# Routed experts on one Trainium2 core: three row tiles an expert, with ten slots for fourth tiles

## The chip, the cores and the metric

The kernel runs on one core of one Trainium2 chip. The metric is the device time of one execution in microseconds. Three runs of the kernel before gave 2011.19, 2011.19 and 2011.78; the median is 2011.19. The profile comes from one further execution.

## The reference

3125 nodes with 256 features go through four residual layers: a three-layer graph attention, a routed expert layer, a graph sum, and a top-1 expert layer. Only the second is touched by the change:

```python
logits = jnp.einsum('bsd,de->bse', x, gate_w) + gate_b          # 16 experts
probs = jax.nn.softmax(logits, axis=-1)
top_probs, top_idx = jax.lax.top_k(probs, 2)                    # two experts a node
top_probs = top_probs / jnp.sum(top_probs, axis=-1, keepdims=True)
h1 = jnp.einsum('bsd,edh->bseh', x, w1)                         # 256 -> 512
h2 = jnp.einsum('bsd,edh->bseh', x, w2)
hidden = jax.nn.silu(h1) * h2
expert_out = jnp.einsum('bseh,eho->bseo', hidden, w3)           # 512 -> 256
```

The output is the sum of each node's two expert outputs with their weights, added to `x`. Each node counts twice, so 6250 rows are spread over 16 experts, on average 390.6 an expert.

## The kernel before

**Routing.** During the last attention layer `Router` computes every group's gates and scatters each normalised row, with its node number and its weight in two further columns, to its expert's place in the DRAM table `rows0` (3200 rows are set aside for each expert). The first 512 rows of every expert are filled beforehand with spare rows (`spare_rows`), whose node number points to spare rows behind `sums`; so an expert may be read as four full tiles of 128 whatever its count is. `Router.finish` takes the largest count to `over`; if an expert had more than 512 rows (`CAP0`), the kernel would run a general path at its end instead.

**Experts.** `routed_experts` loops over the 16 experts and treats all four tiles (`nq = 4`) of one at once:

- ACT's queue issues the loads of w1, w2 and w3 (512 KB each, L692 to L696, two buffers of each); SP's queue issues `xs`, the expert's 512 rows (L700, two buffers).
- DVE casts the node numbers to `who` (L702, two buffers). PE turns `xs` by eight transposes (L707), ACT copies them to `xsT` (L708).
- For each of four 128-wide quarters `j` of the hidden layer, PE multiplies w1 and then w2 with 512 columns of `xsT` (L715) into the PSUM tiles `ps_h1` and `ps_h2` (two buffers each). ACT takes the silu of the first (L718), DVE multiplies by the second into `hid` (L719).
- For each of the four row tiles PE multiplies `hid` with w3 (L723), DVE scales by the row's weight into `y` (L726, three buffers), and POOL issues an indirect DMA that adds the 128 rows into `sums` in DRAM at the rows in `who` (L728).

All products are float32, which PE runs as two passes each. The order of the instructions on an engine is made by the framework from the program's order and its estimates; the queues keep it. An instruction that waits on a semaphore holds up all behind it on its engine, DMA issues on ACT and SP included. In the order that was made, the cast `who` of an expert stands on DVE two experts ahead: the buffer it writes becomes free when the scatter-adds of the expert just finished have landed, and the first `hid` of the next expert stands behind it.

**After it**, the rows of `sums` are read back into `x` (L733) when all scatters have landed, and the graph sum begins. The last stage (`routed_top1`) reads 128-row tiles at places taken from a small table by register loads (L882, L884) and multiplies them (L895 transposes, L868 products); it is the model for the slots of the change and is itself not changed.

Of the kernel before, what the change touches and what calls it, by code (L numbers as in the profile page):

```python
# [9 lines left out]
F32 = mybir.dt.float32  # L10
F16 = mybir.dt.float16
BF16 = mybir.dt.bfloat16
I32 = mybir.dt.int32
# [8 lines left out]
P = 128  # L22
# [498 lines left out]
CAP0 = 512  # L521
CAP1 = 1024
# [20 lines left out]
def table(nc, pool, behind, func):  # L543

    one = pool.tile([P, 1], F32, name="table")
    nc.scalar.activation(one, behind[:, 0:1], func, scale=0.0, bias=1.0)
# [8 lines left out]
class Router:  # L555
# [6 lines left out]
    def __init__(self, tc, cp, ident, eps, iota, count, rows, sums, gate_w, gate_b):  # L562
        nc = self.nc = tc.nc
        self.tc, self.ident, self.eps, self.iota, self.rows, self.sums = tc, ident, eps, iota, rows, sums
# [105 lines left out]
    def finish(self, pp, over):  # L670

        total = pp.tile([1, NX0], F32, name="ps_z")
        self.nc.tensor.matmul(total, self.every[:, 0:1], self.pre[:, NT], start=True, stop=True)
        self.nc.vector.tensor_reduce(over, total, AX.X, OP.max)


def routed_experts(tc, x, ident, rows, sums, w1, w2, w3):
# [6 lines left out]
    nq = CAP0 // P  # L684
    with tc.tile_pool(name="rw", bufs=2) as ep, tc.tile_pool(name="rx", bufs=2) as xp, \
         tc.tile_pool(name="rs", bufs=3) as sp, \
# [3 lines left out]
        for e in range(NX0):  # L690
            a = ep.tile([P, KD, HID0], F32, name="w1")
            nc.scalar.dma_start(a, w1[e].rearrange("(k p) h -> p k h", p=P))  # L692
            b = ep.tile([P, KD, HID0], F32, name="w2")
            nc.scalar.dma_start(b, w2[e].rearrange("(k p) h -> p k h", p=P))
            o = ep.tile([P, nh, D], F32, name="w3")
            nc.scalar.dma_start(o, w3[e].rearrange("(k p) f -> p k f", p=P))  # L696
            xs = xp.tile([P, nq, ROW0], F32, name="xs")
            for q, n in ((0, nq),) if e else ((0, 1), (1, 1), (2, nq - 2)):
                at = e * NP + q * P
                nc.sync.dma_start(xs[:, q:q + n], rows[at:at + n * P].rearrange("(q p) f -> p q f", p=P))  # L700
            who = xp.tile([P, nq], I32, name="who")
            nc.vector.tensor_copy(who, xs[:, :, D])  # L702
            xsT = xp.tile([P, KD, CAP0], F32, name="xsT")
            for k in range(KD):
                ps = tp.tile([P, CAP0], F32, name="ps_x")
                for q in range(nq):
                    nc.tensor.transpose(ps[:, q * P:(q + 1) * P], xs[:, q, k * P:(k + 1) * P], ident)  # L707
                nc.scalar.copy(xsT[:, k], ps)  # L708
            hid = xp.tile([P, nh, CAP0], F32, name="hid")
            for j in range(nh):  # L710
                p1 = pp.tile([P, CAP0], F32, name="ps_h1")
                p2 = pp.tile([P, CAP0], F32, name="ps_h2")
                for ps, w in ((p1, a), (p2, b)):
                    for k in range(KD):
                        nc.tensor.matmul(ps, w[:, k, j * P:(j + 1) * P], xsT[:, k], start=(k == 0),  # L715
                                         stop=(k == KD - 1))
                s = sp.tile([P, CAP0], F32, name="silu")
                nc.scalar.activation(s, p1, AF.Silu)  # L718
                nc.vector.tensor_tensor(hid[:, j], s, p2, op=OP.mult)  # L719
            for q in range(nq):  # L720
                ps = po.tile([P, D], F32, name="ps_o")
                for j in range(nh):
                    nc.tensor.matmul(ps, hid[:, j, q * P:(q + 1) * P], o[:, j], start=(j == 0),  # L723
                                     stop=(j == nh - 1))
                y = sp.tile([P, D], F32, name="y")
                nc.vector.tensor_scalar(y, ps, xs[:, q, D + 1:D + 2], None, op0=OP.mult)  # L726

                independent(tc, f"sums{e}", nc.gpsimd.indirect_dma_start(  # L728
                    out=sums[:, :], out_offset=bass.IndirectOffsetOnAxis(ap=who[:, q:q + 1], axis=0),
                    in_=y, in_offset=None, bounds_check=NP + CAP0 - 1, oob_is_err=True, compute_op=OP.add))  # L730
        table(nc, sp, s, AF.Sqrt)
# [239 lines left out]
def dense_attention(tc, dram, counts, x_in, big, ident, eps, layers, src, dst, rows, high, make_router, over):  # L971
# [10 lines left out]
    with tc.tile_pool(name="dw", bufs=1) as cp, tc.tile_pool(name="dwl", bufs=2) as wl, \  # L982
# [9 lines left out]
        with tc.tile_pool(name="dp", bufs=8) as pmp, tc.tile_pool(name="ds", bufs=2) as sp, \  # L992
# [147 lines left out]
            router.finish(zp, over)  # L1140
# [283 lines left out]
def spare_rows(tc, cp, rows0, rows1):  # L1424
# [16 lines left out]
    to.append((rows1[NX1 * NP:], empty1))  # L1441
    return [lambda o=o, i=i: nc.sync.dma_start(o, i) for o, i in to], [empty0[:, 0, 0:1], empty1[:, 0:1]]
# [3 lines left out]
def routed(ctx: ExitStack, tc: tile.TileContext, i: dict, out: bass.AP, over):  # L1446
# [5 lines left out]
    rows0 = dram.tile([NX0 * NP, ROW0], F32, name="rows0")  # L1452
# [4 lines left out]
    early = ctx.enter_context(tc.tile_pool(name="early", bufs=1))  # L1457
    with tc.tile_pool(name="counts", bufs=1) as kp:
# [3 lines left out]
                                                            i["L0_ffn_gate_w"], i["L0_ffn_gate_b"]), over[:, 0:1])  # L1462
        with tc.tile_pool(name="s0", bufs=1) as sp:
            ws, wm = (two_halves(nc, sp, i["L1_gnn_" + n], "s_" + n) for n in "WM")
            hidden = hidden_weights(nc, early, *(i["L1_ffn_" + n] for n in ("W1", "b1", "Wg", "bg")), x[:, 0, 0:1])
            routed_experts(tc, x, ident, rows0, sums, *(i["L0_ffn_" + n] for n in ("w1", "w2", "w3")))
# [95 lines left out]
```

## Time and profile before

| | |
|---|---|
| median of 3 runs | 2011.19 us (2011.19 to 2011.78) |
| the profiled execution: its time | 2013.53 us |
| its span, and mean granted TensorE clock | 2011.8 us, 0.987 |
| the routed-expert stage in it | 1143 to 1501 us |
| busy in this stage of 358 us | PE 352.2, PEld 209.7, POOL 98.1, DVE 76.5, ACT 58.2 us |
| DMA in this stage | 46% of 16 engines, 107 GB/s |

The span is the time from the first to the last instruction of the profiled execution, and its time the whole of that execution; it was 2.34 us slower than the median of the unprofiled runs. PE is TensorE's products and PEld its weight loads, which run beside the products. A group's line gives the line of the kernel, engine, operation, destination and sources, shape, count, busy microseconds, the mean nanoseconds of one, and the idle time before it with what ended it. Ends of matmuls are modelled and one overlaps the next, so the time of a pass is read from start to start.

### The profile page before, as it was taken

How to read it: one execution, taken by the hardware profiler on the slowest of the kernel's cores; microseconds unless marked ns; L12 is line 12 of the kernel's file. 1: busy time of each engine (PE TensorE's matmuls, PEld its weight loads, DVE VectorE, ACT ScalarE, POOL GpSimd, SP SyncE). 2: the span in 40 equal slices, each digit the busy share in tenths (PEclk: the TensorE clock that was granted, in tenths of full speed). 3: DMA queues.
4: the chain of work that ended last, by engine and by line, in shares of the span. 5: the costliest groups of instructions: out<-in, count | busy, mean ns of one | idle time of the engine just before them, and what ended most of it. 6: DMA issues, size and time to landing. Idle time of an engine off the chain costs nothing. (4 is left out here: it accounts for less than half of the span.)

```text
span 2011.8 us, 27108 instructions
## 1 busy us (share of the span) xinstructions
PE 1899.9 (94%) x9234; PEld 1465.1 (73%) x9234; DVE 1004.2 (50%) x2900; ACT 756.7 (38%) x2242; POOL 287.1 (14%) x398
## 2 busy tenths in 40 slices
PE   2999999999999999999999699999989999997998
PEld 1788888887888888788888356556647887554887
DVE  5888978785444444577777322122226222323222
ACT  2867867672011111122222211111116999544221
POOL 1200000000000000032222223222320000132222
PEclk9999999999999999999999799999999999998999
DMA  4001112476000000111111345545531000633664
GB/s 127 25 1 64 33 64 116 191 281 259 30 0 1 1 1 6 37 43 43 43 43 39 126 110 124 133 105 125 118 60 47 1 1 1 220 157 143 199 208 132
DMA packets 97568, 173.82 MB, mean 86 GB/s; under 512 B 9814, under 2 KB 70581, under 8 KB 97392
## 3 DMA queue, kind: packets, MB, share of 16 engines
q1 hardware_dynamic: 59292, 109.03, 15.8%
q0 software_dynamic: 17264, 35.33, 6.7%
q10 hardware_dynamic: 20866, 27.63, 4.7%
q8 instruction: 76, 1.25, 0.3%
q14 instruction: 70, 0.57, 0.1%
HBM read 82.98 MB, written 91.35 MB: 87 GB/s over the span
## 5 line engine op out<-in xcount | busy, mean ns | idle before, releaser
L1089 PE MATMUL acc<-big,pm 128*128 128x257 f32 (+1 forms) x3750 | 868.1, 382 | 2.5 <-DVE pm L1086 2.1
L1089 PEld LDWEIGHTS acc<-big,pm 128*128 128x128 f32 (+1 forms) x3750 | 681.5, 187 | 108.9 <-DVE pm L1086 7.3
L1086 DVE SCALAR_TENSOR_TENSOR pm<-tau,rho,counts 128x256 f32<-128x256 f32 (+1 forms) x975 | 432.3, 469 | 137.0 <-PE acc L1089 135.1
L715 PE MATMUL ps_h<-xsT,w 128*128 128x512 f32 x512 | 226.5, 601 | 4.0 <-ACT xsT L708 4.0
L715 PEld LDWEIGHTS ps_h<-xsT,w 128*128 128x128 f32 x512 | 96.9, 192 | 124.3 <-issue 111.8
L1206 PE MATMUL acc<-msg,cr 128*128 128x512 f32 (+1 forms) x625 | 157.8, 404 | 0.0
L1405 DVE TENSOR_TENSOR ohk<-iota_k,key 128x1200 f16<-128x1200 f16 x196 | 152.4, 778 | 2.4 <-PE acc_c L1417 2.3
L1417 PE MATMUL acc_c<-ohk,ohs 128*128 128x200 f16 x1176 | 133.3, 251 | 4.9 <-DVE ohs L1405 2.4
L1202 ACT ACTIVATE cr<-counts 128x256 fp32r<-128x256 uint8 (+1 forms) x325 | 130.5, 402 | 19.3 <-DMA sums<-y,who 11.5
L728 POOL DMA_INDIRECT sums<-y,who x64 | 99.3, 1552 | 264.3 <-DVE y L726 249.6
L1206 PEld LDWEIGHTS acc<-msg,cr 128*128 128x128 f32 (+1 forms) x625 | 114.9, 185 | 28.9 <-ACT cr L1202 1.2
L1417 PEld LDWEIGHTS <-ohs 128*128 128x128 f16 x1176 | 105.9, 99 | 29.7 <-DVE ohs L1405 4.2
L1401 ACT ACTIVATE far<-iota_s,low 128x128 f16<-128x128 f16 x360 | 123.7, 398 | 6.3 <-DVE low L1373 1.8
L868 PE MATMUL ps_y<-t_wd,hsT 128*128 x512 | 118.4, 385 | 0.0
L723 PE MATMUL ps_o<-w,hid 128*128 128x256 f32 x512 | 113.1, 379 | 0.0
L723 PEld LDWEIGHTS ps_o<-w,hid 128*128 128x128 f32 x512 | 97.3, 190 | 20.1 <-issue 7.7
L1420 ACT CAST counts<-acc_c 128x400 uint8<-128x400 f32 x196 | 94.0, 479 | 45.4 <-PE acc_c L1417 44.6
L868 PEld LDWEIGHTS ps_y<-t_wd,hsT 128*128 128x128 f32 x512 | 96.5, 194 | 12.3
L718 ACT ACTIVATE silu<-ps_h 128x512 f32<-128x512 f32 x64 | 38.2, 597 | 162.7 <-PE ps_h L715 162.7
L719 DVE TENSOR_TENSOR hid<-silu,ps_h 128x512 f32<-128x512 f32 x64 | 43.8, 688 | 104.9 <-PE ps_h L715 104.8
L777 PE MATMUL ps_H<-big,t_w 128*128 128x512 f32 (+1 forms) x224 | 93.1, 552 | 0.7 <-ACT H L779 0.5
L1071 ACT ACTIVATE tau<-ps_m 128x256 f32<-128x256 f32 (+1 forms) x39 | 14.1, 371 | 209.0 <-PE ps_m L1069 201.0
(242 smaller groups left out, 1772.0 us busy)
## 6 DMA issues: line engine op xcount, KB each, us to landing
rows<-empty SPq DMA_DIRECT2D x16, 2564.0 KB, 9.8
w<-in_L_ffn_w_dram ACTq DMA_DIRECT2D x48, 512.0 KB, 4.3
hs<-rows SPq DMA_DIRECT2D x31, 641.0 KB, 4.2
rows<-empty SPq DMA_DIRECT2D x16, 516.0 KB, 4.2
t_wd<-in_L_ffn_Wd_dram SPq DMA_DIRECT2D x8, 1024.0 KB, 10.8
xs<-rows SPq DMA_DIRECT2D x15, 516.0 KB
bias<-in_L_ffn_bd_dram SPq DMA_DIRECT2D x32, 128.0 KB
big<-in_x_dram SPq DMA_DIRECT2D x6, 512.0 KB
```

What stands on the lines that cost most here:

```text
L715: nc.tensor.matmul(ps, w[:, k, j * P:(j + 1) * P], xsT[:, k], start=(k == 0), stop=(k == KD - 1))
L723: nc.tensor.matmul(ps, hid[:, j, q * P:(q + 1) * P], o[:, j], start=(j == 0), stop=(j == nh - 1))
L728: independent(tc, f"sums{e}", nc.gpsimd.indirect_dma_start(out=sums[:, :], out_offset=bass.IndirectOffsetOnAxis(ap=who[:, q:q + 1], axis=0 ...
L868: nc.tensor.matmul(ps, hsT[:, j], d[:, ds(e, 1), j, :].rearrange("p o f -> p (o f)"), start=(j == 0), stop=(j == nh - 1))
L1086: nc.vector.scalar_tensor_tensor(pm[:, :n], tau[:, :n], now.rho[:, s:s + 1], edges[:, s, :n], op0=OP.max, op1=OP.mult)
L1089: nc.tensor.matmul(acc[:r, j, :D + 1], pm[:, q:q + r], now.h[:, s], start=(s == 0), stop=(s == NT - 1))
L1202: nc.scalar.activation(cr[:, :n], edges[:, s, :n], AF.Copy, accum_out=seen[:, a * NT + s:a * NT + s + 1])
L1206: nc.tensor.matmul(acc[:r, j].rearrange("p h d -> p (h d)"), cr[:, q:q + r], msg[:, s].rearrange("p h d -> p (h d)"), start=(s == 0), stop ...
L1401: nc.scalar.activation(far[:, i], self.iota_s, AF.Abs, scale=-1.0, bias=self.low32[:, pair, i:i + 1])
L1405: nc.vector.tensor_tensor(to[:, i:].rearrange("p t (x u) -> p t x u", u=2), iota.rearrange("p (x u) -> p x u", u=2)[:, None].to_broadcast( ...
L1417: nc.tensor.matmul(acc[:, u], ohs[:, i], ohk[:, i], start=(t == 0), stop=(t == TW - 1))
L1420: nc.scalar.copy(to[:, :, d0 % PAIR:d0 % PAIR + 2 * WIN].rearrange("p s (u d) -> p u s d", u=2), acc.rearrange("p u (s d) -> p u s d", d=WIN))
```

## The change

An expert now reads and multiplies three row tiles (`EACH = 3`, 384 columns). A fourth tile, where an expert has over 384 rows, is done in one of ten slots (`MORE`). `Router.finish` works out from the counts which expert each slot serves and where its rows are, and leaves both in the table `more`; a slot without use takes the last expert's weights and a spare tile at the end of `rows0`. If more than ten experts needed one, `over` would send the kernel to the general path. The slots stand in the iterations of experts 3 to 12, one each; all ten always run.

The loop is also put in a new order: the turning of the next expert's rows stands ahead of `second`, and the slot's first products between `first` and `second`, its second product behind. The slot's loads are all on SP's queue, with an address from a register. w1 and w2 now have three buffers each, shared between experts and slots in turn, w3 two in the same way.

In the order that the framework makes of it, PE runs `first` of an expert, two transposes of the slot, three of the next expert, one product of `second`, the slot's 16 first products, the other three transposes, the rest of `second`, then `second_more`. On ACT, w3 of the next expert stands behind the last copy of `xsT` and waits for the end of `second`; then come w1 of the expert after that, the next silu, and w2. On SP the order is `xs` of two experts on, register load, `xs1`, register load, w1, w2, w3 of the slot. On DVE it is the three `y`, the slot's `y`, `who` of two experts on, `who1` of the next slot, and the four `hid` of the next expert.

The diff, cut to its core:

```diff
+EACH = 3
+MORE = 10
@@ Router.finish
+        end = cp.tile([1, 5, 2 * NX0], F32, name="more_end")
+        nc.vector.memset(end, 0.0)
+        nc.vector.tensor_scalar(end[:, 0, NX0:], total, float(EACH * P), None, op0=OP.is_gt)
+        for j in range(4):
+            nc.vector.tensor_tensor(end[:, j + 1, NX0:], end[:, j, NX0:], end[:, j, NX0 - (1 << j):-(1 << j)],
+                                    op=OP.add)
...
+        nc.vector.tensor_scalar(table[:, 0], slot, float(NX0 - 1), None, op0=OP.min)
+
+        nc.vector.tensor_scalar(slot, slot, float(NP), float(EACH * P), op0=OP.mult, op1=OP.add)
+        nc.vector.tensor_scalar(table[:, 1], slot, float(NX0 * NP), None, op0=OP.min)
@@ routed_experts
-    nq = CAP0 // P
-    with tc.tile_pool(name="rw", bufs=2) as ep, tc.tile_pool(name="rx", bufs=2) as xp, \
-         tc.tile_pool(name="rs", bufs=3) as sp, \
+    nq = EACH
+    with tc.tile_pool(name="rw", bufs=3) as ep, tc.tile_pool(name="rx", bufs=2) as xp, \
+         tc.tile_pool(name="rs", bufs=2) as sp, tc.tile_pool(name="ry", bufs=3) as yp, \
+         tc.tile_pool(name="rm", bufs=1) as mp, tc.tile_pool(name="rw3", bufs=2) as op_, \
...
+        def turn(e):
+            xs = xp.tile([P, nq, ROW0], F32, name="xs")
...
+            xsT = xp.tile([P, KD, EACH * P], F32, name="xsT")
+            for k in range(KD):
+                ps = tp.tile([P, EACH * P], F32, name="ps_x")
+                for q in range(nq):
+                    nc.tensor.transpose(ps[:, q * P:(q + 1) * P], xs[:, q, k * P:(k + 1) * P], ident)
+                nc.scalar.copy(xsT[:, k], ps)
+            return xs, xsT
+
+        def fetch(e):
             a = ep.tile([P, KD, HID0], F32, name="w1")
             nc.scalar.dma_start(a, w1[e].rearrange("(k p) h -> p k h", p=P))
             b = ep.tile([P, KD, HID0], F32, name="w2")
             nc.scalar.dma_start(b, w2[e].rearrange("(k p) h -> p k h", p=P))
+            return a, b
+
+        def first(xsT, a, b):
...
-                p1 = pp.tile([P, CAP0], F32, name="ps_h1")
-                p2 = pp.tile([P, CAP0], F32, name="ps_h2")
+                p1 = pp.tile([P, EACH * P], F32, name="ps_h1")
+                p2 = pp.tile([P, EACH * P], F32, name="ps_h2")
...
+        def second(e, xs, hid, o):
+            who = xp.tile([P, nq], I32, name="who")
+            nc.vector.tensor_copy(who, xs[:, :, D])
             for q in range(nq):
...
+        def first_more(slot):
+            e = nc.values_load(places[0:1, 0, slot:slot + 1], engines=(mybir.EngineType.SP,), min_val=0,
+                               max_val=NX0 - 1, skip_runtime_bounds_check_because="min with the last expert")
+            at = nc.values_load(places[0:1, 1, slot:slot + 1], engines=(mybir.EngineType.SP,), min_val=0,
+                                max_val=NX0 * NP, skip_runtime_bounds_check_because="min with the spare tile")
+            xs = mp.tile([P, ROW0], F32, name="xs1")
+            nc.sync.dma_start(xs, rows[ds(at, P)])
+            a = ep.tile([P, KD, HID0], F32, name="w1")
+            nc.sync.dma_start(a, w1[ds(e, 1)].rearrange("o (k p) h -> p (o k) h", p=P))
+            b = ep.tile([P, KD, HID0], F32, name="w2")
+            nc.sync.dma_start(b, w2[ds(e, 1)].rearrange("o (k p) h -> p (o k) h", p=P))
+            o = op_.tile([P, nh, D], F32, name="w3")
+            nc.sync.dma_start(o, w3[ds(e, 1)].rearrange("o (k p) f -> p (o k) f", p=P))
+            xsT = mp.tile([P, KD, P], F32, name="xsT1")
+            ps = tp.tile([P, KD, P], F32, name="ps_x")
+            for k in range(KD):
+                nc.tensor.transpose(ps[:, k], xs[:, k * P:(k + 1) * P], ident)
+            nc.scalar.copy(xsT, ps)
+            p1 = pp.tile([P, nh, P], F32, name="ps_h1")
+            p2 = pp.tile([P, nh, P], F32, name="ps_h2")
+            for ps, w in ((p1, a), (p2, b)):
+                for j in range(nh):
+                    for k in range(KD):
+                        nc.tensor.matmul(ps[:, j], w[:, k, j * P:(j + 1) * P], xsT[:, k], start=(k == 0),
+                                         stop=(k == KD - 1))
+            hid = mp.tile([P, nh, P], F32, name="hid1")
+            for j in range(0, nh, 2):
+                s = sp.tile([P, 2, P], F32, name="silu")
+                nc.scalar.activation(s, p1[:, j:j + 2], AF.Silu)
+                nc.vector.tensor_tensor(hid[:, j:j + 2], s, p2[:, j:j + 2], op=OP.mult)
+            return slot, xs, hid, o
+
+        def second_more(slot, xs, hid, o):
+            ps = po.tile([P, D], F32, name="ps_o")
+            for j in range(nh):
+                nc.tensor.matmul(ps, hid[:, j], o[:, j], start=(j == 0), stop=(j == nh - 1))
+            y = yp.tile([P, D], F32, name="y")
+            nc.vector.tensor_scalar(y, ps, xs[:, D + 1:D + 2], None, op0=OP.mult)
+            who = yp.tile([P, 1], I32, name="who1")
+            nc.vector.tensor_copy(who, xs[:, D:D + 1])
+            independent(tc, f"more{slot}", nc.gpsimd.indirect_dma_start(
...
+        turned = turn(0)
+        for e in range(NX0):
+            a, b = fetch(e)
+            o = op_.tile([P, nh, D], F32, name="w3")
+            nc.scalar.dma_start(o, w3[e].rearrange("(k p) f -> p k f", p=P))
+            xs, xsT = turned
+            hid, s = first(xsT, a, b)
+            more = first_more(e - 3) if 0 <= e - 3 < MORE else None
+            if e + 1 < NX0:
+                turned = turn(e + 1)
+            second(e, xs, hid, o)
+            if more:
+                second_more(*more)
@@ spare_rows
+    to.append((rows0[NX0 * NP:], empty0[:, 0]))
@@ routed
-    rows0 = dram.tile([NX0 * NP, ROW0], F32, name="rows0")
+    rows0 = dram.tile([NX0 * NP + P, ROW0], F32, name="rows0")
+    more = early.tile([1, 2, MORE], I32, name="more")
```

## The prediction

> **What bounds the kernel now.** I read the page first (engine shares, then the groups of the routed-expert lines), then the groups and waits of 1143 to 1501 us alone, which is the stage that changes, then one expert in order of time, then its DMA microsecond by microsecond. The page:
>
> ```profile
> PE 1899.9 (94%) x9234; PEld 1465.1 (73%) x9234; DVE 1004.2 (50%) x2900; ACT 756.7 (38%) x2242; POOL 287.1 (14%) x398
> ...
> L715 PE MATMUL ps_h<-xsT,w 128*128 128x512 f32 x512 | 226.5, 601 | 4.0 <-ACT xsT L708 4.0
> ...
> L723 PE MATMUL ps_o<-w,hid 128*128 128x256 f32 x512 | 113.1, 379 | 0.0
> ```
>
> TensorE is the bound, and inside the stage more so: PE is busy 352.2 of its 358 us and waits 4.0 us in all before the first product. A float32 product is two passes, so an expert has 32 passes of 512 columns and 32 of 256. One expert in order of time (start, length):
>
> ```profile
> 1182.63 0.37 ACTq L692 DMA_DIRECT2D w<-in_L_ffn_w_dram  x1
> 1182.86 0.19 PEld L715 LDWEIGHTS ps_h<-xsT,w 128*128 128x128 f32 x1 [0.24 <-issue]
> 1183.29 0.19 PEld L715 LDWEIGHTS ps_h<-xsT,w 128*128 128x128 f32 x1 [0.24 <-issue]
> 1184.14 7.07 PE L723 MATMUL ps_o<-w,hid 128*128 128x256 f32 x32
> 1190.54 1.55 POOL L728 DMA_INDIRECT sums<-y,who  x1 [0.30 <-issue]
> 1191.05 1.04 PE L707 MATMUL ps_x<-ident,xs 128*128 128x128 f32 x8
> 1192.39 1.55 POOL L728 DMA_INDIRECT sums<-y,who  x1 [0.30 <-issue]
> 1198.34 0.17 DVE L702 CAST who<-xs 128x4 int32<-128x4 f32 x1 [6.60 <-DMA sums<-y,who]
> 1198.44 0.69 DVE L719 TENSOR_TENSOR hid<-silu,ps_h 128x512 f32<-128x512 f32 x1
> 1204.65 0.38 ACTq L692 DMA_DIRECT2D w<-in_L_ffn_w_dram  x1
> ```
>
> The reader is to see three things. The period of an expert is 22.02 us (1182.63 to 1204.65). A 512-column pass takes 0.429 us (start to start of its weight loads). And the first scaled product `hid` of an expert stands on DVE behind `who`, which waits until the scatter-adds of the expert just finished have landed, 5.95 us after the last of them began. That wait is long, but free today:
>
> ```profile
> DVE who L702 <- DMA sums<-y,who: 96.7, 14, 8.0
> PE ps_h L715 <- ACT xsT L708: 4.0, 16, 0.4
> ```
>
> Price of narrower passes, from the last stage, which runs 128-column and 256-column passes of the same kind:
>
> ```profile
> 1840.42 0.97 PEld L777 LDWEIGHTS ps_H<-big,t_w 128*128 128x128 f32 x8 [0.48 <-ACT H L779]
> ...
> 1865.06 0.87 PE ps_cols L895 x8
> 1865.93 3.46 PE ps_y L868 x16
> ```
>
> L777 is the shape of the new narrow product: eight weight loads in 0.97 us, so (0.97 - 0.19) / 7 = 0.111 us per pass of 128 columns. L868 gives 3.46 / 16 = 0.216 us per 256. So 0.111, 0.216, 0.429: time goes with columns, with no floor down to 128, and 384 columns take the midpoint, 0.3225.
>
> **The change, part by part.** (1) Fewer tiles. Before, one expert is 32 x 0.429 = 13.73, 32 x 0.216 = 6.91 and 8 transposes 1.04: 21.68, and 0.34 of waiting to make 22.02; 16 experts 352.3 us. After, an expert of three tiles is 32 x 0.3225 = 10.32, 24 x 0.216 = 5.18, 6 x 0.13 = 0.78: 16.28, times 16 = 260.5. A slot is 2 x 0.13 = 0.26, 32 x 0.111 = 3.55, 8 x 0.216 = 1.73: 5.54, and all 10 slots always run: 55.4. Together 315.9, that is 64 tiles of work become 58. The 0.34 goes too, since `turn` of the next expert now stands ahead of `second`, except at expert 0. Gain 36.0 us.
>
> A rule of the Trainium skill speaks against this: "TensorE: Matmul & The Clock Gate", section "Back-to-back issue gap", gives about 81 ns sustained at 128 columns and 131 at 512, so a quarter of the columns would cost 0.62 of a pass. Scaled to 0.429, a slot's 32 passes would take 8.5 us instead of 3.55 (50 us over ten), and a 384-column pass about 0.373 (26 us over 512 of them): a loss of some 40. The L777 row is this data type, this shape and a stream of loads and passes, so it decides.
>
> (2) The order inside an expert. On PE: `first`, the slot's two transposes, half of the next expert's, one product of `second`, the slot's 32 passes, the other half, `second`, `second_more`. The slot's passes need `xsT1` from ACT (a 128x256 copy took 0.37, L623) and have 0.39 + 0.43 us of PE work to cover it. Nothing is charged; uncovered it would be under 0.5 us a slot.
>
> (3) The wait that moves. Let T be the end of `second`. Where a slot ran, DVE's order is now y of the slot, `who` two experts on, `who1` of the next slot, and then the first `hid` of the next expert. The third scatter starts at T + 1.22 (row 1190.54; 24 passes after 1184.14 end at 1189.32). The 14 waits of the trace end 5.8 to 7.4 us after the last scatter's start, mean 6.2: T + 7.42. With `who` and `who1` 0.1 each and `hid` of 384 columns 0.52 (0.69 x 0.75), `hid` is out at T + 8.14. PE starts the next `first` at T + 1.73 and needs the PSUM pair of its first quarter again for the third's second half: T + 1.73 + 2 x 2.58 + 1.29 = T + 8.18. Before, with 512 columns, the margin was about 0.4 us in the worst case (`hid` out at 1376.71, wanted at about 1377.2); now it is nil. And the scatter meets more traffic:
>
> ```profile
> 1194.00:1195.00 1.00, 1.00 (x3) 0.38 (x2) 0.00 (x0) 0.60 (x1) 0.00 (x0) 1.00 1.11 380
> 1195.00:1196.00 1.00, 1.00 (x4) 0.52 (x3) 0.00 (x0) 0.00 (x0) 0.00 (x0) 1.00 1.17 242
> 1196.00:1197.00 1.00, 1.00 (x4) 0.43 (x3) 0.00 (x0) 0.00 (x0) 0.00 (x0) 1.00 1.08 376
> 1197.00:1198.00 1.00, 1.00 (x3) 0.38 (x2) 0.00 (x0) 0.22 (x1) 0.00 (x0) 1.00 0.96 170
> 1198.00:1199.00 1.00, 1.00 (x4) 0.51 (x3) 0.66 (x2) 0.38 (x1) 0.00 (x0) 1.00 0.00 0
> ```
>
> The last two columns are DMA share and GB/s: after `second` the engines are full for four microseconds at 292 GB/s (w3 and xs, 1.05 MB), and the scatter lands as they run dry. After the change ACT issues w1 of a later expert right behind w3 (+0.52 MB), xs shrinks by 0.13, and the slot's loads follow. If the scatter still lands with the drain: 0.39 MB more, 1.3 us, and PE stalls 1.3 us per boundary. Against it, "DMA: Bandwidth & Descriptors", section "Queues, rings and completion order", says each DMA engine takes turns between queues that have work; then one more load on ACT's queue takes nothing from the scatter's turn and the stall is 0 (total 36 instead of 23). I take 1.0, nearer the row, with 0 and 3 as ends. Ten boundaries: -10 us.
>
> (4) The slot's loads on SP. Its weights queue behind xs of two experts on, which waits for y of the running expert, and behind xs1, whose buffer is free when y of the slot is out (T + 2.5). Two register loads stand between:
>
> ```profile
> L882 SPq TENSOR_LOAD <-table x32: 262/272/365, 1854.6 to 1987.2; - x32
> ```
>
> One 0.27 load is under the wait; the other and three issues of 0.33 put w1 at about T + 3.8. Until w2 of the slot is in, DMA moves 1.57 (three ACT loads) + 0.53 + 1.05 = 3.15 MB, at 0.29 MB/us from T + 2.4: T + 13.3. PE asks for it at T + 1.73 + 10.32 + 1.08 + 1.78 = T + 14.9, later by any stall. Charged nothing; bounds 0 and 1.5 us a slot. On ACT, w3 waits for the end of `second`, and only w1 and a silu that needs later PE work stand behind it. On POOL the slot's scatter waits for the expert's to land, done by about T + 14, before the next is due at T + 19.
>
> (5) The ends. `finish` adds a dozen tiny DVE operations (0.15 each) and an iota; one stands ahead of the last weights: -0.15. The spare tile's fill hides in the attention. w3 of experts 0 and 1 now loads beside the first xs (1140.34), one tile smaller: -0.5 (from -1.5 to +0.4).
>
> Sum: 36.0 - 10 - 0.65 = 25.4 us. The profiled execution (span 2011.8, time 2013.53) would become 1988.1; the median of the three runs is 2.34 us lower, 2011.19, and gives 1985.8.
>
> **Rivals.** (A) No stall: the scatter keeps its turn. Gain 35.4, 1976. For: fair queues, and the waits vary only by 1.6 us today. Against: they end with the drain. (B) Stall of 2 to 3.4 us, or w2 late too: gain 1.5 to 15, about 2003. (C) Slower: the scatter lands behind the slot's w1 and w2. Then 1.57 - 0.52 + 0.53 + 1.05 = 2.62 MB drain at T + 11.4, `hid` is out at T + 12.2, PE stalls 4.0 at ten boundaries, -40, and the time is 2016. It decides from a landing about 9.7 us after the third scatter's start, where the stall is 3.5. Against: the scatter is at work before those loads begin at T + 3.8. (D) The narrow passes have a floor after all, about 2050; L777 speaks against it. That the change does nothing is excluded: shapes and counts are fixed in the program. With this input the reference's routing gives seven experts over 384 rows and 473 at most, so ten slots hold them.
>
> **How the numbers follow.** The forecast 0.50 (1979 to 1996), A 0.28, B 0.13, C 0.07, D 0.02. Likeliest: 1986. The range 1973 to 2000 takes in the forecast, A and part of B. About 0.2%, 4 us, is what a measurement of this kernel can tell from no change: faster 0.88, same 0.03, slower 0.09.
>
> **What would show it.** The product line of `first` at 0.32 us a pass, the slot's at 0.11, a period of 16.3 us without a slot and 22 to 23 with one, TensorE waits of about 1 us on DVE's `hid`, and `who` still waiting on the scatters. Passes of 0.17 or more at 128 columns, waits on the slot's w or xs1, or a period over 25 us would make it wrong.

## The result, and the profile after

| | before | after |
|---|---|---|
| time, median of the runs, us | 2011.19 (2010.70 to 2011.78, 4 runs) | 1994.67 (1992.44 to 1996.39, 4 runs) |
| ratio of the times, 95% interval | | 0.9918 [0.9905, 0.9930] |
| profiled execution: time, span, us | 2013.53, 2011.8 | 1992.44, 1990.5 |
| first `xs` issue to the load of `sums`, us | 1140.34 to 1504.35 | 1138.64 to 1487.13 |
| DMA share and GB/s in the stage | 0.46, 107 | 0.55, 154 |

The change brings 16.5 us, 0.8%; the forecast was 25.4. The time lies in the range of 1973 to 2000, but 9 us above the predicted 1986, at the upper end of the forecast's own 1979 to 1996. Two terms of the sum account for that, and a third, too low, hides part of it.

First what came as forecast. The TensorE timeline of the kernel after, columns start, duration, instruction group, and in brackets the idle time ahead of it with its releaser; first an expert without a slot, then one with:

```profile
1181.62 10.48 PE L746 MATMUL ps_h<-xsT,w 128*128 128x384 f32 x32
1191.94 0.82 PE L728 MATMUL ps_x<-ident,xs 128*128 128x128 f32 x6
1192.59 5.34 PE L759 MATMUL ps_o<-w,hid 128*128 128x256 f32 x24
1197.78 10.48 PE L746 MATMUL ps_h<-xsT,w 128*128 128x384 f32 x32
...
1233.16 3.73 PE L791 MATMUL ps_h<-xsT,w 128*128 128x128 f32 x32
...
1243.54 6.61 PE L746 MATMUL ps_h<-xsT,w 128*128 128x384 f32 x20
1252.29 4.14 PE L746 MATMUL ps_h<-xsT,w 128*128 128x384 f32 x12 [2.14 <-DVE hid L750]
...
1267.62 6.61 PE L746 MATMUL ps_h<-xsT,w 128*128 128x384 f32 x20
1275.82 4.14 PE L746 MATMUL ps_h<-xsT,w 128*128 128x384 f32 x12 [1.58 <-DVE hid L750]
```

From L746 to the next group's start, 32 passes of 384 columns take 1191.94 - 1181.62 = 10.32 us, 0.3225 each; the slot's 32 passes of 128 columns take 3.57 us from start to start (1233.16 to 1236.73, where the next transposes begin), 0.112 each. A plain expert has a period of 16.16 us. An expert with a slot has 24.08 us between 1243.54 and 1267.62 (23.75 on average over nine), 2.14 of them a wait of the first product on `hid`, 20 passes into it.

That wait is the main loss. The waits of the stage, columns total us, times, longest us:

```profile
DVE who L755 <- DMA sums<-y,who: 82.5, 14, 7.6
...
PE ps_h L746 <- DVE hid L750: 17.1, 10, 2.5
...
PE ps_x L728 <- DMA xs<-rows: 3.0, 2, 1.8
...
DVE who L807 <- DMA xs<-rows: 1.2, 5, 0.3
```

And the boundary at 1243.54 on DVE, where one can read what stands ahead of `hid`:

```profile
1243.74 0.48 DVE L805 TENSOR_SCALAR y<-ps_o,xs 128x256 f32<-128x256 f32 x1 [1.24 <-PE ps_o L803]
1251.14 0.17 DVE L755 CAST who<-xs 128x3 int32<-128x3 f32 x1 [6.92 <-DMA sums<-y,who]
1251.60 0.15 DVE L807 CAST who<-xs 128x1 int32<-128x1 f32 x1 [0.29 <-DMA xs<-rows]
1251.68 1.02 DVE L750 TENSOR_TENSOR hid<-silu,ps_h 128x384 f32<-128x384 f32 x2
```

DVE does nothing for 6.92 us, then two casts of 0.15 to 0.17 us, then two `hid` at once: the second was ready as well. The third scatter of the expert had begun at 1243.03, so `who` ran 8.11 us after it. Over the nine boundaries between two slots this distance is 7.5 to 8.8 us, mean 7.96; in the trace of before it was 6.2 after the last scatter. With T = 1241.81, the end of `second`, the prediction's points are all in this trace (third scatter T + 1.22, next `first` T + 1.73), except the landing: T + 7.42 was the base, and T + 9.33 it is.

### The profile page after: what moved, and what is told of

It is laid out like the page before. It is cut to its first block, busy times and chain, and to the rows that moved or that the text cites. A ratio compares the mean times of both kernels' runs of the same rounds, so it can differ in the third digit from the quotient of the medians.

```text
span 1990.5 us, 27914 instructions
## 1 busy us (share of the span) xinstructions
PE 1866.0 (94%) x9494; PEld 1487.9 (75%) x9494; DVE 1002.9 (50%) x2937; ACT 757.3 (38%) x2272; POOL 278.6 (14%) x395
## 5 line engine op out<-in xcount | busy, mean ns | idle before, releaser
L746 PE MATMUL ps_h<-xsT,w 128*128 128x384 f32 x512 | 173.2, 494 | 17.4 <-DVE hid L750 17.1
L746 PEld LDWEIGHTS ps_h<-xsT,w 128*128 128x128 f32 x512 | 97.7, 193 | 87.2 <-DVE hid L750 23.6
L749 ACT ACTIVATE silu<-ps_h 128x384 f32<-128x384 f32 x64 | 31.4, 491 | 224.8 <-PE ps_h L746 186.8
L764 POOL DMA_INDIRECT sums<-y,who x48 | 74.5, 1552 | 188.1 <-DVE y L762 178.4
L759 PE MATMUL ps_o<-w,hid 128*128 128x256 f32 x384 | 87.2, 379 | 0.0
L1202 DVE TENSOR_SCALAR col<-acc 128x2 f32<-128x2 f32 (+1 forms) x39 | 6.1, 157 | 158.7 <-PE acc L1184 158.7
L1056 PE MATMUL ps_m<-we,yT 128*128 128x258 f32 x300 | 80.1, 396 | 5.3 <-ACT yT L1224 2.9
```

The costliest lines, as they stand in the source:

```text
L764: independent(tc, f"sums{e}", nc.gpsimd.indirect_dma_start(out=sums[:, :], out_offset=bass.IndirectOffsetOnAxis(ap=who[:, q:q + 1], axis=0 ...
```

## The experiments

Each kernel starts from the changed one (1994.67) unless it says otherwise. Ratios are to the kernel before, run beside it on the same chip; its medians there lie between 2010.98 and 2011.35, so times of different chips are compared as they stand. One execution of each kernel was traced.

**One cast at a time.** Theory: DVE works in order, and `hid` stands behind two casts that wait for transfers; the one that waits for the scatters, `who`, is the costly one. Rival: the landing of the slot's rows, for which `who1` waits, holds `hid` nearly as long. A third theory is that the landing is long only because of the added loads.

```diff
-            nc.vector.tensor_copy(who, xs[:, :, D])
+            nc.gpsimd.tensor_copy(who, xs[:, :, D])
```

> The cast `who` of `second` moves from DVE to POOL; everything else, `who1` on DVE included, stays as in the changed kernel (1994.67). Main theory: the stall of 1.7 us at the ten boundaries is DVE's order, `hid` behind `who`, which waits for the scatters' landing; `who` starts 7.5 to 8.1 us after the third scatter, 1.5 over what the margin allows. With `who` on POOL only `who1` is left ahead of `hid`. `who1` was held by the landing of xs1 in 5 of 9 cases for 1.2 us in all after `who`, so xs1 lands late in about half of the boundaries, early in the other half: about half of the 17.1 us goes, 1986. Rival 1 (xs1's landing alone holds `hid` nearly as long everywhere): only 0 to 3 us go, 1992 to 1995. If xs1 is early wherever it was not seen: 1981.

Measured: 2006.16 us, ratio 0.9976 [0.9970, 0.9983]. Moving the cast that waits longest made the kernel 11.5 us slower. Waits of this kernel in the stage:

```profile
DVE who L807 <- DMA xs<-rows: 77.0, 10, 10.8
...
PE ps_h L746 <- DVE hid L750: 22.9, 9, 3.2
...
DVE y L805 <- DMA sums<-y,who: 7.8, 3, 3.4
```

The main theory's 1986 fell. The rows of the slot are issued on SP behind three tiles of `xs`, and `who1` ran 5.7 to 8.4 us after that issue, 8.4 after the third scatter on average, so in this kernel its wait alone holds `hid` as long as both did. In three cases the slot's y also waited for a scatter, and in two of them the next slot's rows were issued late for it. The stalls sum to 22.9 instead of 17.1 us. The rest of the loss is in the windows of one microsecond around the second of them (columns: window, length, busy time and instructions of PE, PEld, DVE, ACT and POOL, then granted clock, DMA share, GB/s):

```profile
1250.00:1251.00 1.00, 0.80 (x3) 0.18 (x1) 0.00 (x0) 0.00 (x0) 0.00 (x0) 1.00 1.16 311
1251.00:1252.00 1.00, 0.00 (x0) 0.00 (x0) 0.00 (x0) 0.00 (x0) 0.00 (x0) 1.00 1.09 366
1252.00:1253.00 1.00, 0.00 (x0) 0.00 (x0) 0.50 (x2) 0.00 (x0) 0.00 (x0) 1.00 1.04 400
1253.00:1254.00 1.00, 0.81 (x3) 0.55 (x4) 0.60 (x2) 0.49 (x1) 0.61 (x1) 1.00 1.07 412
1254.00:1255.00 1.00, 1.00 (x4) 0.57 (x3) 0.00 (x0) 0.00 (x0) 1.00 (x2) 0.66 1.04 388
1255.00:1256.00 1.00, 1.00 (x3) 0.50 (x2) 0.50 (x1) 0.00 (x0) 0.14 (x1) 0.50 1.14 339
```

PE stands still for 2.4 us, starts again, and 1.1 us later the granted clock falls to 0.50, for about 3.4 us. The 12 passes behind this stall take 5.83 us where they take 4.14 at full clock. It happened after three of the nine stalls, those of 2.40, 2.68 and 2.87 us, and costs 3 x 1.69 = 5.1 us. With 5.8 us of longer stalls that is 10.9 of the 11.5, and the traces agree: from the router's last product to the load of `sums` this one takes 365.01 us, 10.93 more than that of the changed kernel. The 5.1 us are no property of the edit alone: they depend on when a stall falls (last section).

```diff
-            nc.vector.tensor_copy(who, xs[:, D:D + 1])
+            nc.gpsimd.tensor_copy(who, xs[:, D:D + 1])
```

> The cast `who1` of `second_more` moves from DVE to POOL; `who` stays on DVE. Main theory: `who`, with its wait for the scatters, is the larger part, so only the 1.2 us of waits for xs1 and ten casts of 0.15 go: 1992. Rival 1 (xs1's landing is what holds `hid`): 10 us or more go, 1984 or less.

Measured: 1995.78 us, ratio 0.9932 [0.9916, 0.9949]; no change that can be told from the changed kernel. `PE ps_h L746 <- DVE hid L750` is 15.1 us in 10 waits here, against 17.1. The rival's 1984 or less fell, and the main theory's 1992 is 4 us away, but for a reason that e1 shows: each of the two waits suffices alone.

**Both casts.**

> Both casts move from DVE to POOL. Main theory: nothing on DVE waits for a DMA ahead of `hid` any more, the ten stalls (17.1 us in the profile) go but for a few tenths each: 1977 to 1979, and the TensorE wait on `hid` of the first product falls below 2 us. Rival 2 (the stall comes from something else that ends at that moment, or the next thing is late: w1 or w2 of the slot, the slot's rows): a wait of 1 us or more at each boundary appears elsewhere, 1985 to 1990. If POOL's own order, with the scatters now queued behind a waiting cast, is the new limit: `second_more`'s scatter late, y's buffers late, 1985 or more.

Measured: 1975.20 us, ratio 0.9834 [0.9818, 0.9851]. The same kernel ran once more, beside e9 (below):

> The kernel with both casts on POOL a second time, beside e9 on one chip: 1975.2, and 2 us over e9 if the theory on the start holds.

Measured: 1973.52 us, ratio 0.9818 [0.9805, 0.9832]. The whole stall is gone. TensorE timeline of two boundaries:

```profile
1218.54 10.48 PE L746 MATMUL ps_h<-xsT,w 128*128 128x384 f32 x32
...
1240.21 10.48 PE L746 MATMUL ps_h<-xsT,w 128*128 128x384 f32 x32
...
1261.89 3.39 PE L746 MATMUL ps_h<-xsT,w 128*128 128x384 f32 x10
```

No idle time in brackets, 32 passes in one run (the last line is cut by the end of the window), and a period of 21.67 us with a slot. POOL of the same kernel:

```profile
1240.19 1.55 POOL L764 DMA_INDIRECT sums<-y,who  x1 [0.30 <-issue]
1248.57 1.55 POOL L808 DMA_INDIRECT sums<-y,who  x1 [6.83 <-DMA sums<-y,who]
1249.56 0.75 POOL L755 CAST who<-xs 128x3 int32<-128x3 f32 x1
1249.69 0.74 POOL L807 CAST who<-xs 128x1 int32<-128x1 f32 x1
```

The scatters land no sooner (8.38 us from the third one's start to the slot's), and the casts, which overlap the slot's scatter and each other here, last 0.75 and 0.74 us; with no scatter right ahead (at 1172.26) the same cast took 0.19 on POOL, and on DVE it takes 0.17. Both are free, because POOL's next work comes at 1257.67. What counted was who stands behind the wait. The gain is also larger than the 17.1 us of waits: 24.08 - 2.14 = 21.94 us is a period without its wait, and 21.67 is what it is without the stall. A product stream cut in two takes 6.61 + 4.14 = 10.75 us instead of 10.48, so each break costs 0.27 us on top of its idle time, 2.7 over ten. 17.1 + 2.7 = 19.8, and 1994.67 - 1975.20 = 19.5 (21.2 with the second measurement; from the router's last product to the load of `sums` the two traces are 20.6 and 19.6 us shorter).

**The slot's loads.** The slots use w1, w2, w3 of the running expert, so thirty loads of 0.52 MB are gone. The order of the engines was meant to stay; on DVE it did not quite, as is shown below:

```diff
-        def first_more(slot):
-            e = nc.values_load(places[0:1, 0, slot:slot + 1], ...)
+        def first_more(slot, a, b, o):
...
-            a = ep.tile([P, KD, HID0], F32, name="w1")
-            nc.sync.dma_start(a, w1[ds(e, 1)]...)
...
-            more = first_more(e - 3) if 0 <= e - 3 < MORE else None
+            more = first_more(e - 3, a, b, o) if 0 <= e - 3 < MORE else None
```

> The ten slots load no weights: they use w1, w2 and w3 of the running expert, and the register load of the slot's expert goes. The slot's rows are then multiplied by another expert's weights; its thirty loads of 0.52 MB are what is left out. The order on every engine stays. It also frees the third buffer of w1 and w2 for the plain experts. Main theory in the form of rival 2 (the landing is stretched by the added DMA work): `who` starts about 6.2 us after the third scatter as before, the stall falls to about 0.1 to 0.3, 1977 to 1980. If the order alone is to blame and the landing stays at 7.5 to 8: 1992 to 1995. If w1 of the later expert, which ACT issues right behind w3, is the added load that matters: stall about 1, 1987.

Measured: 1979.32 us, ratio 0.9853 [0.9836, 0.9869]. Waits of the stage (the slot's cast is L799 in this kernel):

```profile
DVE who L755 <- DMA sums<-y,who: 67.3, 14, 6.3
...
PE ps_h L746 <- DVE who L799: 1.9, 2, 1.1
PE ps_h L746 <- DVE hid L750: 0.9, 1, 0.9
```

With both casts still on DVE, 2.8 us of stall are left, in three of ten boundaries. From the third scatter's start to `who` it is 5.8 to 7.5 us, mean 6.5 over the nine boundaries between slots. So the cause has two halves, and taking either away leaves next to nothing of the stall: the order puts `hid` behind the landing, and loads move the landing from 6.5 to 8.0 us, past the margin. Which loads, this kernel can't say. Without tiles of their own the slots don't turn the buffers over, and ACT issues only w3 at a slot's boundary (1242.76), not w1 and w2 of a later expert as the changed kernel does (1242.47 and 1245.09). Two more kernels keep the buffers and cut one set of loads to a quarter each. First the slots' (and the same for w2 and w3):

```diff
-            nc.sync.dma_start(a, w1[ds(e, 1)].rearrange("o (k p) h -> p (o k) h", p=P))
+            nc.sync.dma_start(a[:, :, :P], w1[ds(e, 1), :, 0:P].rearrange("o (k p) h -> p (o k) h", p=P))
...
-                        nc.tensor.matmul(ps[:, j], w[:, k, j * P:(j + 1) * P], xsT[:, k], start=(k == 0),
+                        nc.tensor.matmul(ps[:, j], w[:, k, :P], xsT[:, k], start=(k == 0),
```

> The slots keep their own tiles of w1, w2, w3 and all their instructions, but load only the first quarter of each (0.13 MB instead of 0.52) and use it four times; the rows of the slots get no proper product. The rotation of the buffers stays, so ACT still issues w1 and w2 of a later expert at the slot's boundary, which it did not do when the slots had no tiles of their own. Theory S (the slot's own loads lengthen the landing): `who` about 6.5 us after the third scatter instead of 8.0, stall below 0.5 a boundary, 1977 to 1982. Theory W (w1 of the later expert, right behind w3, is the added load that counts, as the prediction had it): the landing stays at 7.5 or more, 1990 or more. Both in part: 1983 to 1990.

Measured: 1996.81 us, ratio 0.9927 [0.9911, 0.9944]. Then w1 and w2 of the experts, on ACT, in `fetch` (the same for w2), with products in `first` that use the quarter four times:

```diff
-            nc.scalar.dma_start(a, w1[e].rearrange("(k p) h -> p k h", p=P))
+            nc.scalar.dma_start(a[:, :, :P], w1[e, :, 0:P].rearrange("(k p) h -> p k h", p=P))
```

> The mirror image: the slots load all of their weights, and ACT loads only the first quarter of w1 and w2 of each expert, which the expert uses four times; the experts' first products are not the proper ones. Theory S: the landing stays at 7.5 to 8, 1990 or more, less about 2 for an earlier start. Theory W: `who` about 6.5 us after the third scatter, 1976 to 1982. If either reduction alone is enough to bring the landing to 6.5, the loads are exchangeable and only their sum counts.

Measured: 1980.63 us, ratio 0.9846 [0.9829, 0.9862]. The waits of e11, and then those of e12:

```profile
DVE who L755 <- DMA sums<-y,who: 80.5, 14, 7.7
...
PE ps_h L746 <- DVE hid L750: 17.7, 10, 2.5
```

```profile
DVE who L755 <- DMA sums<-y,who: 71.0, 14, 6.6
...
PE ps_h L746 <- DVE who L807: 2.6, 4, 0.7
...
PE ps_h L746 <- DVE hid L750: 1.4, 1, 1.4
```

Cutting 1.2 MB of the slot's loads leaves the landing at 7.85 us (mean of nine) and the stall at 17.7. Cutting 0.8 MB of the expert's brings it to 6.6 us and the stall to 4.0. Theory W holds: what ACT issues behind w3 while the scatters are starting counts; what SP issues from 1245.15 on, two microseconds after the third scatter's start (1243.03), does not. Whether w1 alone would do can't be told, since w2 was cut with it; w2 is issued at 1245.09, as late as SP's first.

Two things beside this have to be known. In e4 and e12 the framework put `who1` behind the first `hid` at all nine boundaries, so that one wait less stood ahead of it; in e11 and the changed kernel it stands ahead. DVE in e12:

```profile
1245.73 0.17 DVE L755 CAST who<-xs 128x3 int32<-128x3 f32 x1 [5.92 <-DMA sums<-y,who]
1245.84 0.56 DVE L750 TENSOR_TENSOR hid<-silu,ps_h 128x384 f32<-128x384 f32 x1
1246.31 0.15 DVE L807 CAST who<-xs 128x1 int32<-128x1 f32 x1
```

This can account for little of the gain: e2, which has `who` alone ahead of `hid` and the loads uncut, keeps 15.1 us of stall. And the loads that count differ from the others in their queue as well as in their time. One boundary tells these apart. Before the first slot's rows are multiplied, that slot's w3 is issued on SP, 1.02 us ahead of the third scatter (1197.97 and 1198.99 in the changed kernel), and ACT issues nothing there; `who` runs 5.73 us after the scatter. In e11 this load is a quarter:

```profile
1196.70 0.35 SPq L780 DMA_DIRECT2D w<-in_L_ffn_w_dram  x1
...
1197.73 1.55 POOL L764 DMA_INDIRECT sums<-y,who  x1 [0.30 <-issue]
1202.01 0.17 DVE L755 CAST who<-xs 128x3 int32<-128x3 f32 x1 [2.09 <-DMA sums<-y,who]
```

Now it is 4.28 us. In e4, where the load at this place is a whole one on ACT, it is 5.74. So a load on SP delays the landing too if it is issued ahead of the scatter: by this boundary it is the time that decides and not the queue.

**Order alone, and tiles alone.**

```diff
-EACH = 3
+EACH = 4
...
-    with tc.tile_pool(name="rw", bufs=3) as ep, ...
+    with tc.tile_pool(name="rw", bufs=2) as ep, ...
...
-            more = first_more(e - 3) if 0 <= e - 3 < MORE else None
+            more = None
```

> Four row tiles in every expert as in the kernel before, no slots, w1 and w2 with two buffers as before; kept from the change are the new order (`turn` of the next expert ahead of `second`), the cast `who` inside `second` and w3 in a pool of its own. Main theory: the order alone brings the 0.34 us of `xsT` wait at 15 boundaries, 5 us, and no stall on `hid`, since `who` stands behind the first `hid` on DVE here: 2006 to 2009, the higher end if the start is as late as in the changed kernel (2.4 us). If the order of the experts matters more than that, or if a wait on `hid` shows without any slot, the slots are not the cause of the stall: 2015 or more, or 2000 or less.

Measured: 2004.68 us, ratio 0.9963 [0.9950, 0.9976], 6.4 us faster than the kernel before on that chip (2011.08) and a little below what was expected. TensorE timeline, two starts of an expert:

```profile
1191.19 13.90 PE L746 MATMUL ps_h<-xsT,w 128*128 128x512 f32 x32
...
1212.70 13.90 PE L746 MATMUL ps_h<-xsT,w 128*128 128x512 f32 x32
```

The period is 21.51 us, against 22.02 before: 0.51 a boundary, of which the wait for `xsT` was 0.25 (4.0 us in 16 waits); the other 0.26 is about the 0.27 that a break in the stream costs. Over 15 boundaries that is 7.7 us, less 0.9 for a later first product. No product waits for `hid`. So 6 to 7 of the 16.5 us come from the new order of the loop, in which `turn` stands ahead of `second`, not from fewer tiles.

The next one has three tiles everywhere and no slots, and leaves out the rows above 384:

```diff
-            more = first_more(e - 3) if 0 <= e - 3 < MORE else None
+            more = None
```

> Three row tiles in every expert and no slots at all: the rows above 384 of seven experts are left out. It prices the ten slots. Main theory: a slot costs 5.5 us of TensorE work, 1.7 us of stall and 0.27 us for breaking the product stream in two, 7.5 us together, so 1994.67 - 75 = 1920, with a period of 16.16 us at every expert and no wait on `hid`. If a stall remains without slots, or if the slots were cheaper than that: above 1925.

Measured: 1920.15 us, ratio 0.9548 [0.9535, 0.9560], on the expected 1920. Ten slots cost (1994.67 - 1920.15) / 10 = 7.45 us each, and with both casts on POOL (1975.20 - 1920.15) / 10 = 5.5. The two are the price of a slot with and without its stall, and 5.51 is also the difference of the periods in e3, 21.67 - 16.16.

**The start of the stage.** From the router's last product (L678, before L673) to the first product of expert 0 it was 1134.51 to 1145.78, 11.27 us; after the change it is 13.41:

```profile
1133.05 0.17 PE L678 MATMUL ps_z<-pre,every 128*1 128x16 bf16 x1 [0.27 <-DVE g_place L654]
1141.10 0.66 PE L728 MATMUL ps_x<-ident,xs 128*128 128x128 f32 x2 [7.88 <-issue]
1143.56 0.69 PE L728 MATMUL ps_x<-ident,xs 128*128 128x128 f32 x2 [1.80 <-DMA xs<-rows]
1145.42 0.69 PE L728 MATMUL ps_x<-ident,xs 128*128 128x128 f32 x2 [1.17 <-DMA xs<-rows]
1146.46 13.32 PE L746 MATMUL ps_h<-xsT,w 128*128 128x384 f32 x32 [0.36 <-ACT xsT L729]
```

The second and third tile of `xs` come late, and w3 of experts 0 and 1 is issued beside them. The pool of w3 opened first lets w3 load earlier:

```diff
-    with tc.tile_pool(name="rw", bufs=3) as ep, tc.tile_pool(name="rx", bufs=2) as xp, \
+    with tc.tile_pool(name="rw3", bufs=2) as op_, tc.tile_pool(name="rw", bufs=3) as ep, \
+         tc.tile_pool(name="rx", bufs=2) as xp, \
...
-         tc.tile_pool(name="rm", bufs=1) as mp, tc.tile_pool(name="rw3", bufs=2) as op_, \
+         tc.tile_pool(name="rm", bufs=1) as mp, \
```

> The changed kernel with the pool of w3 opened first, so that w3 of experts 0 and 1 lie where nothing of the router lies and load before its row scatters are done, not beside the first xs. Main theory: the two waits for the second and third xs tile (1.8 and 1.2 us) shrink to what the kernel before had, the first product comes 5.4 us after the first xs issue instead of 7.8: 1992.3. Rival: xs is late for its own reasons (three tiles in three transfers), and nothing changes: 1994.7.

> Both casts on POOL and the pool of w3 first. Main theory: the two repairs add up, 1975.2 - 2.4 = 1972.8, no TensorE wait on `hid` in the stage and a first product 5.4 us after the first xs issue. Rival (the start's wait is not w3's): 1975.

Measured: 1996.15 us, ratio 0.9934 [0.9918, 0.9950], and with both casts on POOL 1975.51, ratio 0.9824 [0.9811, 0.9837]. No gain. The waits for the second and third tile are gone, but the first `xs` is now issued at 1142.90 instead of 1138.64 (e7), since the router's row scatters landed later, and the first product stands 13.58 and 13.49 us behind the router's last. The bytes had only changed places. The suspicion left was the third buffer of w1 and w2: with it eight loads of 0.52 MB are on their way ahead of the first product, and before there were six. So w1 and w2 of expert 2 were made to wait for the first rows, on top of e8:

```diff
+        first_rows = turned[0][:, nq - 1, 0:1]
...
+            if late is not None:
+                nc.vector.tensor_copy(a[:, 0, 0:1], late)
...
-            a, b = fetch(e)
+            a, b = fetch(e, first_rows if e == 2 else None)
```

(and the same for `b`).

> Both casts on POOL and w3's pool first, and now w1 and w2 of expert 2 (1.05 MB) wait until the third row tile of expert 0 has landed: one element of each is first written by DVE from that tile. Theory after e7 and e8 (the start is late because three buffers of w1 and w2 let 1.05 MB more pass the DMA engines ahead of the first xs, wherever w3 stands): the first product comes 11.3 us after the router's last product, as in the kernel before, and not 13.5: 1973.3. Rival (the start's loss lies in the new operations of `finish` or in the three separate xs transfers): 13.5 stays, 1975.5.

Measured: 1972.41 us, ratio 0.9806 [0.9793, 0.9820].

```profile
1134.11 0.17 PE L678 MATMUL ps_z<-pre,every 128*1 128x16 bf16 x1 [0.27 <-DVE g_place L654]
1142.73 1.51 PE L729 MATMUL ps_x<-ident,xs 128*128 128x128 f32 x6 [8.45 <-DMA xs<-rows]
1145.18 13.29 PE L751 MATMUL ps_h<-xsT,w 128*128 128x384 f32 x32 [0.94 <-ACT xsT L730]
```

The first product is back at 11.07 us behind the router's last, and the theory's 11.3 holds. In time it is 1.1 us less than both casts alone on that chip (1973.52), which the intervals don't tell from nothing; the trace shows the two microseconds, the times don't settle them. The step from e8 (13.49 to 11.07) is the third pair's alone. That the place of w3 counts for nothing is not shown by it: e5, with two pairs of w1 and w2 and w3 beside the first rows (four tiles of them), has 12.20. This is the fastest of the kernels that do the whole work, 22 us below the changed one, and all but 1 to 3 of these come from the two casts.

## Why the prediction was right or wrong

| term of the sum | predicted, us | measured, us |
|---|---|---|
| (1) fewer tiles, `xsT` wait gone | 36.0 | 38.3 |
| (3) stall, ten boundaries | -10 | -19.8 |
| (5) start and `finish` | -0.65 | -2.1 |
| sum | 25.4 | 16.4 |

The measured gain is 16.5. The profiled pair nearly agrees: from the router's last product to the load of `sums` it is 369.84 us before and 354.08 after, 15.8 us. Its spans differ by more, 21.3; the rest lies outside the stage. The profiled execution of before was 2.3 us above its median, and the router's last product came 1.5 us earlier after; in two runs of one kernel (e3 and e10) it also came 1.2 us apart.

- **(1) Passes by columns: right.** 0.3225 and 0.112 us against 0.3225 and 0.111. The figures of the Trainium skill, "TensorE: Matmul & The Clock Gate", section "Back-to-back issue gap", from which the estimate was a loss of 40 us, don't hold for this data type and stream; taking the row of the same shape was right. The small excess: a plain expert has 16.16 us instead of 16.28, a slot 5.51 instead of 5.54, so 352.3 - (16 x 16.16 + 10 x 5.51) = 38.6, less 0.3 for expert 0. The prediction's sums of passes run a little high: four tiles make 21.68 us, where e5 has a period of 21.51, so its 0.34 us of waiting was partly a break in the stream.
- **(2) The copy of `xsT1`: right.** The slot's products have no idle time ahead of them in the kernel after.
- **(3) The wait that moves: right in its place and its cause, too small.** The stall is on `hid`, behind `who` and `who1`, at the 21st pass, in all ten boundaries (in the last, with no `who1`, it is only 0.80 us), and e12 shows its cause as the prediction had it: w1 (with w2) of a later expert behind w3. The failed term is the 1.0 us a boundary, chosen between 1.3 (the scatter lands when the engines run dry) and 0 (each queue keeps its turn); 1.71 was measured, and the period with a slot left the 22 to 23 us that were given for it. The landing rose by 7.96 - 6.2 = 1.76. Put that into the prediction's line and `hid` is out at T + 9.90, where PE wants it at T + 8.18: 1.72 late; the measured mean is 1.71. Two smaller terms were missing. A break in the product stream costs 0.27 us beyond its wait, 2.7 in all. And `who1` was entered as 0.1 us of work, though it has a wait of its own, which costs as much where `who` is out of the way (e1).
- **The queue rule: on the wrong side.** Turns between queues, as the Trainium skill has them ("DMA: Bandwidth & Descriptors", section "Queues, rings and completion order"), were read to mean that one more load on ACT's queue takes nothing from the scatter. It took 1.3 us or more (6.64 against 7.96). The section speaks of turns packet by packet and gives no time for a small transfer beside large ones; the reading went beyond it. The row that speaks of the full engines was the better guide, and going below its 1.3 toward the rule was an error. But not for the reason given: the scatter doesn't land as the engines run dry. In the changed kernel they move 411 GB/s in the microsecond of the landing (1251 to 1252) and run dry in 1256 to 1257, five later.
- **(4) The slot's loads: right.** w2 was forecast at T + 13.3; its issue at 1245.73 and a median of 9.0 us to landing, over the ten slots, give T + 12.9. PE first asks for it later and never waits, in e3 neither, where PE comes 2 us sooner.
- **(5) The start: outside its ends.** -0.5 was put for w3 beside the first `xs`, and -2.1 it is. The prediction looked at w3; e8 and e9 show that it is the third pair of w1 and w2, which it had only as a load in later boundaries. What w3's place would cost without that pair stays open, 12.20 in e5 against 11.07 in e9 being an upper end. The 0.15 for `finish` is too small to be found.
- **The rivals.** A (no stall, 1976) is what e3 gives, 1975, once nothing waits in front of `hid`. C (2016, the scatter lands behind the slot's w1 and w2) is refuted by e11: those loads hardly move the landing. e1 came nearest to it, 2006, by another way, a longer wait and a halved clock. B's stall of 2 us or more was there in three of ten boundaries. D is excluded by the passes.

## What to carry to other kernels

Before loads are moved next to a wait that is free today, work out its margin: here it was nil, and w1 and w2 of a later expert, issued behind w3 while the scatters started, cost ten stalls, while half as many bytes again, issued two microseconds later, cost nothing. A small cast that waits for a transfer belongs on an engine with nothing urgent behind it: up to 0.75 us on POOL was cheaper than 0.17 on DVE. If two waits stand ahead of the same instruction, take both away before judging, since one alone showed nothing or worse.

## What the runs showed of the hardware that was not expected

- A TensorE pause of 2 to 3 us can halve the granted clock for 3.4 us, soon after work has started again: after pauses of 2.40, 2.68 and 2.87 us in e1 (12 passes in 5.83 us instead of 4.14), of 2.04 in e11 and of 2.17 in e7, but not after 2.77 and 3.20 us in e1, nor after any of the kernel after, up to 2.47. The length of the pause doesn't decide; its place in time does. In e1's trace the clock changes twelve times between 1124.62 and 1861.90, always a whole multiple of 3.413 us apart, to 0.01 us: the clock is set in fixed steps of that length. Lay these steps over the pauses on `hid` of the kernel after, e1, e7 and e11 (39 of them). The five that were followed by a fall have 2.01 to 2.45 us of idle time inside one step, and the fall is that step's end. The 34 others have at most 1.90: the pause of 3.20 us (1375.54 to 1378.74) has a step's end at 1377.21 in it and is split into 1.67 and 1.53. In these traces a fall thus takes some 2 us of idle time within one step; no run moved a pause on purpose to try it.
- From the third scatter's start to its landing it is 5.7 us at a plain boundary (6.4 at the first), where ACT issues w3 and SP `xs`, and 8.0 (up to 8.8) where ACT issues w1 as well. The slot's loads on SP, started 2 us later, leave the landing as it is, whole or cut to a quarter (7.96 and 7.85), though the engines move 299 to 411 GB/s from 1245 to 1254 with the whole ones. A load that SP issued 1 us ahead of the scatter did count: 5.73 us with 0.52 MB, 4.28 with 0.13, in one boundary.
- Fewer bytes ahead brought the first rows sooner, an earlier place did not: w3 moved earlier delayed the row scatters by as much as it gave back (e7), and 1.05 MB held back on top of that gained 2 us (e9).
